# The gate and up product of a block by seven products of halves, with running sums in PSUM

## The chip, the cores and the metric

The kernel runs on one core of one Trainium2 chip. The metric is the device time of one launch in microseconds (us), as the median of several runs. The engines are TensorE (PE: matmuls; its weight loads are shown apart as PEld), VectorE (DVE), ScalarE (ACT), GpSimd (POOL) and SyncE (SP), which issues most of the DMA transfers. Everything is float32 except the grid of quantized values, which is bfloat16. A float32 matmul appears as two records on PE.

## The reference

The input is x of shape 4 x 2048 x 256. All of it is normalized, and two branches work on the normalized xn; their results are multiplied.

```python
xn = _layernorm(x)
# s: a linear attention layer
Q = elu(xn @ Wq + bq) + 1;  K = elu(xn @ Wk + bk) + 1;  V = xn @ Wv + bv     # 16 heads of 64
KV = einsum('bshd,bshm->bhdm', K, V)
Z = 1 / (einsum('bshd,bhd->bsh', Q, K.sum(axis=1)) + 1e-6)
o = einsum('bshd,bhdm,bsh->bshm', Q, KV, Z)
x1 = layer_norm(xn + o @ Wo + bo, g1, be1)
s = layer_norm(x1 + gelu(x1 @ W1 + b1) @ W2 + b2, g2, be2)
# g: a gated feed-forward layer whose operands are quantized to FP4 in blocks of 16
fp4_linear = lambda x, w: fp4_quant_dequant(x) @ fp4_quant_dequant(w).T
h = silu(fp4_linear(xn, w_gate)) * fp4_linear(xn, w_up)     # 704 wide
g = silu(fp4_linear(h, w_down))
out = x + s * g
```

A block of 16 values is quantized by its greatest magnitude: scale = max / 6, each value over the scale is rounded to the nearest of 0, 0.5, 1, 1.5, 2, 3, 4, 6, and multiplied by the scale again. The keys and values of a whole batch are needed before its first row of attention.

## The kernel before

**Blocks.** The 8192 rows are 32 blocks of 256 rows (`TB` = 2 halves of 128 rows, `j` = 0, 1), eight to a batch. The first part of the program reads the weights, quantizes those of the gated layer and works through the keys of batch 0. The main loop runs over the blocks n = 0 to 31. While the blocks of one batch are worked on, two sub-blocks of the keys of the next batch go along with each (`keys_k`, `keys_xk`): this holds for n = 0 to 23, the last batch (n = 24 to 31) has no such work. In the first half of a batch the keys' rows are normalized in the block before, in the second half they are loaded again from DRAM. Program step n multiplies the gate and up product of block n + 1 (`gate_up(n + 1)`, L753), because the quantization that must follow it takes most of a block.

**One block in order of TensorE.** Keys of the next batch (`pk`, `pxk`), then the gate and up product (`pg`), the down product of block n (`pd`), the first part of the second feed-forward product of block n - 1 (`py`) or more keys, the attention product (`pa`), the rest of the keys and of `py`; in between, the transposes of x1 (`pt_x`) and of the scales (`pscale`); then the queries of block n + 1 (`pq`), the first feed-forward product (`pf`) and the row sums of attention (`pz`). TensorE and all queues of DMA follow the program's order. ScalarE and VectorE instructions of the loop are placed by a scheduler that runs ahead of the launch; `tc.issue_after(x)` holds an instruction behind x. In the launch the order of each engine is fixed.

**The gate and up product** (`gate_up`, L753 to L776). The left side is the quantized xn of a block, transposed: `qT[:, NI + c, j*128 : (j+1)*128]` is the half c of the 256 contracted values, for the row half j. The right side `wgu` (L339) holds both weights side by side, 1408 columns for each c. For each j and each piece of 352 columns (`IH`), a gate tile and an up tile are accumulated over c = 0, 1: 16 matmuls of 128x352 in eight tiles of PSUM. ScalarE takes silu of the gate tile into h, VectorE multiplies h by the up tile. `mm_tile` (L89) gives out PSUM banks from a rotating pool of four (tag "mm"), `acc_tile` (L92) from a pool of two.

**After it.** `qz` (L865) multiplies the queries by the normalizing factor zb, in two halves of VectorE. zb comes through DRAM: `sums` (L838) writes the reciprocal z (`z_d`) and loads it four times, spread over partitions. The four loads are in SP's queue, behind what was issued before. `qz` is held behind `blk[n + 1]["late"]`, the third of the four multiplications that make h. Then `attention_sums` (the sums `zs`), the attention product `pa` and `add_seven` give x1, in `attention_norm` (L966) its statistics go to POOL for the power of -1/2 (L430) and x1 is normalized, and TensorE transposes it (`x1_T`, L971). In the last batch `pa` is a plain product, and x1 one add.

**The quantization of h** has a reduction of magnitudes (`scales_h`), its reciprocal and a multiplication (`fp4_scaled`), a magnitude by ScalarE (`m_h`), a rounding and a subtraction into `grid` (`fp4_rounded`), for each half j; `grid_T` transposes the grid by DMA, `spread_scales` sends the scales through DRAM to `qT`, and in the next step `quantized_h` and `quantized_x` multiply the two in `qT`.

**Seven products.** The attention and the second feed-forward product are already made by seven products of halves instead of eight (`seven_sums`, `seven_products`, `add_seven`, L889 to L922): sums of quarters of the left side, sums of quarters of the weights, each of the seven products in its own part of two banks, and the results added by VectorE.

**Values and keys of a half** (`m_of_half`, L608). Twice per batch, the sums of keys over 512 columns are multiplied by Wv (`wv`) and Wo. wv is loaded from DRAM or, for one half, kept from the first part in a tile of its own (`wv_sb`, L252).

Of the kernel before, what the change touches and what calls it, by code (L numbers as in the profile page):

```python
# [8 lines left out]
F32 = mybir.dt.float32  # L9
# [3 lines left out]
ALU = mybir.AluOpType  # L13
AX = mybir.AxisListType

P = 128
# [6 lines left out]
def linear_attention_gated_by_fp4_ffn(  # L23
# [230 lines left out]
    def load_wv(f, dep):  # L254
        wv_sb[f] = batch.tile([P, ND, HALF], F32, tag="wv", name=f"wv_{f}", bufs=1)
        load_when(dep, wv_sb[f], by_chunks(Wv)[:, :, f * HALF : (f + 1) * HALF])

    def wv_bias(f):
        bias_in_row0("v", wv_sb[f], f, nc.gpsimd)
        wv_d[f] = dram.tile([P, ND, HALF], F32, tag=f"wv_d{f}", name=f"wv_d{f}", bufs=1)  # L260
        nc.sync.dma_start(wv_d[f], wv_sb[f])
        if f > 0:
            del wv_sb[f]
# [75 lines left out]
    wgu = const.tile([P, ND, 2 * I], F32, name="wgu")  # L339
# [31 lines left out]
    def quantize_gu(ks):  # L371
# [14 lines left out]
        for i, k in enumerate(ks):  # L386
            pt = mm_tile(f"pwgu_{k}")
            for c in range(ND):
                lo = i * D + c * P
                tr(pt[:, c * P : (c + 1) * P], w[:, lo : lo + P], ident)  # L390
            scalar.copy(
                wgu[:, :, k * P : (k + 1) * P], pt[:, : ND * P].rearrange("p (c k) -> p c k", c=ND)
            )
# [214 lines left out]
    def m_of_half(b, f, dep=None, ahead=False):  # L608
# [3 lines left out]
        if wv_sb.get(f) is not None:  # L612
            wv = wv_sb.pop(f)
        else:
            wv = batch.tile([P, ND, HALF], F32, tag="wv", name=f"wv_{nm}", bufs=1)
            nc.sync.dma_start(wv, wv_d[f])
# [9 lines left out]
        xk = batch.tile([P, ND, HALF], F32, tag="xk", name=f"xk_{nm}", bufs=1)  # L626
# [115 lines left out]
    def quantized_x(n):  # L742

        qx = qT[:, NI:, :]
        t = gridT[n][:, NI * TB :, :].rearrange("p (c j) t -> p c (j t)", j=TB)
        return vector.tensor_tensor(qx, qx, t, ALU.mult)
# [6 lines left out]
    def gate_up(n):  # L753
        blk[n]["h"] = []
        for j in range(TB):
            h = work.tile([P, I], F32, tag="h", name=f"h_{n}_{j}")
            blk[n]["h"].append(h)
            for i in range(2):
                halves = []
                for part in range(2):  # L760
                    pg = mm_tile(f"pg_{n}_{j}_{i}_{part}")[:, :IH]
                    lo = part * I + i * IH
                    for c in range(ND):
                        mm(
                            pg, qT[:, NI + c, j * P : (j + 1) * P], wgu[:, c, lo : lo + IH],
                            start=c == 0, stop=c == ND - 1,
                        )
                    halves.append(pg)
                    if part == 0:
                        yield  # L770
                hh = h[:, i * IH : (i + 1) * IH]
                scalar.activation(hh, halves[0], AF.Silu)
                ins = vector.tensor_tensor(hh, hh, halves[1], ALU.mult)
                if (j, i) == (1, 0):
                    blk[n]["late"] = ins.ins
                yield  # L776
# [288 lines left out]
    for n in range(NB):  # L1065
# [52 lines left out]
        if n == 6:  # L1118
            load_xn(0)
# [10 lines left out]

    step(gate, 4)
    step(ready)
    step(m_0)
    scales_h(0, 0)
    scales_x(1)
    step(gate, 4)
# [33 lines left out]
    for n in range(NBLK):  # L1170
# [79 lines left out]
        if subs:  # L1250
            keys_xk(b + 1, subs[1])
            if subs[1] % NB == NB - 1:
                m_half = m_of_half(b + 1, subs[1] // NB)
                step(m_half)
# [29 lines left out]
        if n > 0:  # L1284
            ffn_2(n - 1, 28)
        if more[0]:
            q_of(n + 1)
# [74 lines left out]
```

## Time and profile before

| | before |
|---|---|
| median of 3 runs | 1878.16 us (1877.71 to 1878.72) |
| span of the profiled execution | 1880.7 us |
| granted clock of TensorE | 0.999 |
| PE busy | 1861.7 us, 99% |
| PEld (weight loads) busy | 1383.0 us, 74% |
| DVE busy | 1363.6 us, 73% |
| ACT busy | 706.7 us, 38% |
| POOL busy | 386.9 us, 21% |
| gate and up product, PE rows `pg` | 308.5 us in 1024 records |

The profile shows one execution, whose span of 1880.7 us stands 2.5 us above the median of the runs. A line of a group of instructions names the line of the kernel, the engine, the operation, the tile written and the tiles read, the number of instructions, then their busy time, the mean duration of one in ns, and the engine's idle time just before them with what ended it. L103 and L119 are the helpers through which all matmuls and all scheduled instructions of VectorE and ScalarE pass, so a group is known by its tiles. A line of the waits gives the waiting engine and tile, what it waited for, and then the total, the number of waits and the longest, in us. A line of the timeline gives start and duration in us, the engine, and how many instructions are merged into it; brackets give idle time before it and its releaser. Instructions on VectorE overlap slightly, so the pitch from one start to the next is a little shorter than a duration.

### The profile page before, as it was taken

Reading aid. Unit: us, or ns where it says so; the run is one execution under the profiler, and the core shown is the slowest. Engines: PE = TensorE matmul, PEld = TensorE weight load, DVE = VectorE, ACT = ScalarE, POOL = GpSimd, SP = SyncE. Lnnn points to the kernel's source line nnn. Section 1 sums busy time; section 2 is a strip of 40 time slices with the busy share of each in tenths; the row PEclk is TensorE's granted clock in tenths of the full one; section 3 lists DMA queues with packets and bytes.
Section 4 is the critical chain, followed back from the end, with each engine's and each line's share of the span. In section 5 each row is a group of like instructions: output and inputs, shape, how many; then the busy total and the mean of one; then the engine's idle time right before and its main releaser. Section 6 shows DMA issues by size and latency. Waiting matters only on the chain.

```text
span 1880.7 us, 25219 instructions
## 1 busy us (share of the span) xinstructions
PE 1861.7 (99%) x9324; PEld 1383.0 (74%) x9324; DVE 1363.6 (73%) x2526; ACT 706.7 (38%) x1191; POOL 386.9 (21%) x371
## 2 busy tenths in 40 slices
PE   9999999999999999999999999999999999999998
PEld 4456677777777777777677787777777788888887
DVE  5676777766677877777667787776676767777775
ACT  2333544333334335443233533353322333333332
POOL 1411322011122212220112221122101122222212
PEclk9999999999999999999999999999999999999999
DMA  5526564434535456635344544564543544444442
GB/s 184 193 73 130 117 124 103 96 101 94 96 64 94 115 98 122 143 66 111 80 89 79 117 100 103 96 139 87 95 86 72 104 75 87 82 90 83 88 84 54
DMA packets 229434, 188.78 MB, mean 100 GB/s; under 512 B 107687, under 2 KB 191155, under 8 KB 229310
## 3 DMA queue, kind: packets, MB, share of 16 engines
q1 hardware_dynamic: 228476, 185.58, 47.4%
q8 instruction: 74, 1.21, 0.3%
q10 hardware_dynamic: 834, 1.58, 0.3%
q14 instruction: 50, 0.41, 0.1%
HBM read 131.96 MB, written 32.59 MB: 87 GB/s over the span
## 4 chain that ended last, share of the span: by engine, by line
PE 78%; DVE 11%; DMA 7%; issue 1%; POOL 1%; SPq 1%; ACT 1%; POOLq 0%; ACTq 0%; DVEq 0%
PE pg L103 13%; PE pf L103 11%; PE pk L103 10%; PE pxk L103 10%; PE pq L103 9%; PE pa L103 8%; PE pd L103 7%; PE py L103 7%; DMA zb<-z_d 3%; PE pz L103 2%; DMA z_d<-z 1%; DVE y L119 1%; DMA xn<-xn_d 1%; DVE x L119 1%; DVE hs L119 1%
## 5 line engine op out<-in xcount | busy, mean ns | idle before, releaser
L430 POOL TENSOR_TENSOR rstd<-rstd,neg_half 128x2 f32<-128x2 f32 (+1 forms) x98 | 77.8, 795 | 1298.0 <-DVE rstd L119 984.9
L103 PE MATMUL pg<-wgu,qT 128*128 128x352 f32 x1024 | 308.5, 459 | 0.1
L103 PEld LDWEIGHTS pg<-wgu,qT 128*128 128x128 f32 x1024 | 194.3, 190 | 113.7 <-issue 11.5
L103 PE MATMUL pk<-wk_sb,xnT_k 128*128 128x512 f32 x512 | 230.4, 592 | 1.2 <-ACT xnT_k L119 1.2
L103 PE MATMUL pq<-xnT,wq_sb 128*128 128x256 f32 x1024 | 227.6, 380 | 1.5 <-DVE zq L119 1.4
L103 PE MATMUL pxk<-kk,xn_k 128*128 128x512 f32 x496 | 227.9, 598 | 1.0 <-DVE kk L119 1.0
L103 PE MATMUL pf<-x1T,w_sb 128*128 128x256 f32 x1024 | 227.2, 380 | 1.1 <-DVE zq L119 0.6
L103 PEld LDWEIGHTS pf<-x1T,w_sb 128*128 128x128 f32 x1024 | 193.8, 190 | 30.4 <-DVE zq L119 4.0
L103 PEld LDWEIGHTS pq<-xnT,wq_sb 128*128 128x128 f32 x1024 | 191.8, 190 | 27.7 <-DVE zq L119 3.1
L119 DVE SCALAR_TENSOR_TENSOR kk<-ek,pk 128x512 f32<-128x512 f32 x128 | 85.6, 685 | 173.2 <-ACT ek L119 173.2
L103 PE MATMUL pd<-wd,qT 128*128 128x256 f32 x768 | 172.9, 380 | 0.0
L103 PEld LDWEIGHTS pk<-wk_sb,xnT_k 128*128 128x128 f32 x512 | 97.0, 190 | 102.6 <-issue 89.0
L119 ACT ACT_TABLE_LOAD x121 | 155.2, 1283 | 40.9 <-PE pk L103 26.0
L119 ACT ACTIVATE x1T<-pt_x,bcol 128x256 f32<-128x256 f32 x64 | 32.7, 561 | 359.3 <-PE pt_x L106 359.3
L103 PEld LDWEIGHTS pd<-wd,qT 128*128 128x128 f32 x768 | 145.3, 190 | 26.4 <-issue 2.5
L103 PEld LDWEIGHTS pxk<-kk,xn_k 128*128 128x128 f32 x496 | 89.4, 190 | 99.1 <-issue 87.3
L119 DVE TENSOR_TENSOR h<-h,pg 128x352 f32<-128x352 f32 x128 | 66.1, 517 | 107.1 <-PE pg L103 104.0
L119 ACT ACTIVATE h<-pg 128x352 f32<-128x352 f32 x128 | 58.9, 460 | 209.8 <-PE pg L103 209.7
L119 ACT ACTIVATE hT<-pf,bcol 128x256 f32<-128x256 f32 x256 | 106.1, 472 | 66.7 <-PE pf L103 66.3
L119 DVE TENSOR_TENSOR zq<-zq,zb 128x1024 f32<-128x1024 f32 x64 | 78.9, 1232 | 68.9 <-DMA zb<-z_d 68.8
L103 PE MATMUL py<-w_sb,hs 128*128 128x128 f32 x992 | 122.0, 275 | 0.0
L119 ACT ACTIVATE e<-pq,neg_one 128x512 f32<-128x512 f32 x128 | 86.2, 685 | 83.7 <-PE pq L103 71.2
(161 smaller groups left out, 2777.8 us busy)
## 6 DMA issues: line engine op xcount, KB each, us to landing
zb<-z_d SPq DMA_DIRECT2D x128, 256.0 KB, 6.2
qT<-scale_d SPq DMA_DIRECT2D x248, 128.0 KB, 6.0
x_k<-in_L_attn_src_dram SPq DMA_DIRECT2D x32, 256.0 KB, 4.1
x<-in_L_attn_src_dram SPq DMA_DIRECT2D x32, 256.0 KB, 2.9
xn_d<-xn_k SPq DMA_DIRECT2D x32, 256.0 KB, 2.5
xn<-xn_d SPq DMA_DIRECT2D x32, 256.0 KB, 2.7
xnT_d<-xnT_k SPq DMA_DIRECT2D x32, 256.0 KB, 2.0
xnT<-xnT_d SPq DMA_DIRECT2D x32, 256.0 KB, 4.3
```

The source lines that it names most:

```text
L103: return tc.keep_in_program_order(nc.tensor.matmul(*args, **kw))
L119: ins = op(*args, **kw)
L430: pool["last"] = nc.gpsimd.tensor_tensor(rstd[:, j0:j1], rstd[:, j0:j1], neg_half[:, j0:j1], ALU.pow).ins
```

## The change

The product of a block is written as a product of 2 x 2 quarters: the left side has row halves and halves of the contracted values (`quarters_of`), the right side halves of the contracted values and gate or up, each 704 columns wide. Seven products of quarters replace eight, each for two pieces of 352 columns, 14 matmuls in place of 16. The left sides 3, 5, 6, 7 are sums `xs` that VectorE makes once a block, in a tile that shares its place with x1T. The sums of the weights (`gate_sums`) are made once by POOL; `wgu` keeps seven parts in place of four, and the copies into it are split at the border between gate and up.

The products are put together in PSUM where several outputs share a partial sum: two banks (`run`) hold product 1, ScalarE copies it out as the base of the gate's first half, product 6 is added onto it, ScalarE copies that out as the base of up, product 7 is added onto it, and at last product 4, which makes the gate's second half. A second pair of banks holds product 5, which ScalarE copies out, and then product 5 plus 3. A third allocation of two banks takes product 2. VectorE adds the pieces (`up`, in a tile that shares its place with `zs`). ScalarE takes silu of the first half of h from SBUF and of the second from PSUM. Both halves of h are complete only at the end of the product; `late` is now the last multiplication of the first half.

To make room, wv is no longer kept: each `m_of_half` loads it into a tile that it shares with xk and with zb, and the start's copy of Wv uses the tile of wo. `m_of_half` moves behind the last part of `ffn_2`, and in the first part the order of the last weight, the first gate product and the scales of x is changed.

```diff
@@ -252,15 +252,13 @@
     wv_sb, wv_d = {}, {}
 
     def load_wv(f, dep):
-        wv_sb[f] = batch.tile([P, ND, HALF], F32, tag="wv", name=f"wv_{f}", bufs=1)
+        wv_sb[f] = batch.tile([P, ND, HALF], F32, tag="wo", name=f"wv_{f}", bufs=1)
         load_when(dep, wv_sb[f], by_chunks(Wv)[:, :, f * HALF : (f + 1) * HALF])
 
     def wv_bias(f):
         bias_in_row0("v", wv_sb[f], f, nc.gpsimd)
         wv_d[f] = dram.tile([P, ND, HALF], F32, tag=f"wv_d{f}", name=f"wv_d{f}", bufs=1)
-        nc.sync.dma_start(wv_d[f], wv_sb[f])
-        if f > 0:
-            del wv_sb[f]
+        nc.sync.dma_start(wv_d[f], wv_sb.pop(f))
 
     cols = {}
 
@@ -336,7 +334,18 @@
         return x.rearrange("p (k e) -> p k e", e=BLK)
 
 
-    wgu = const.tile([P, ND, 2 * I], F32, name="wgu")
+    wgu = const.tile([P, 7, I], F32, name="wgu")
+    GU_OF = {"11": 0, "21": 1, "t1": 2, "22": 3, "t2": 4, "t3": 5, "t4": 6}
+
+    def wg(q):
+        return wgu[:, GU_OF[q], :]
+
+    def gate_sums():
+        nc.gpsimd.tensor_tensor(wg("t3"), wg("22"), wg("t1"), ALU.subtract)
+        nc.gpsimd.tensor_tensor(wg("t1"), wg("t1"), wg("11"), ALU.subtract)
+        nc.gpsimd.tensor_tensor(wg("t2"), wg("22"), wg("t1"), ALU.subtract)
+        nc.gpsimd.tensor_tensor(wg("t4"), wg("21"), wg("t2"), ALU.subtract)
+
     wd = const.tile([P, NI, D], F32, name="wd")
     nc.gpsimd.memset(wd[TAIL:, NI - 1, :], 0.0)
 
@@ -388,9 +397,15 @@
             for c in range(ND):
                 lo = i * D + c * P
                 tr(pt[:, c * P : (c + 1) * P], w[:, lo : lo + P], ident)
-            scalar.copy(
-                wgu[:, :, k * P : (k + 1) * P], pt[:, : ND * P].rearrange("p (c k) -> p c k", c=ND)
-            )
+            ptc = pt[:, : ND * P].rearrange("p (c k) -> p c k", c=ND)
+            lo, hi = k * P, (k + 1) * P
+            for part in range(2):
+                a, z = max(lo, part * I), min(hi, (part + 1) * I)
+                if a < z:
+                    scalar.copy(
+                        wgu[:, part * ND : (part + 1) * ND, a - part * I : z - part * I],
+                        ptc[:, :, a - lo : z - lo],
+                    )
         yield
 
     def load_down():
@@ -609,11 +624,9 @@
 
 
         nm = f"{b}_{f}"
-        if wv_sb.get(f) is not None:
-            wv = wv_sb.pop(f)
-        else:
-            wv = batch.tile([P, ND, HALF], F32, tag="wv", name=f"wv_{nm}", bufs=1)
-            nc.sync.dma_start(wv, wv_d[f])
+        t = work.tile([P, 2, ND, HALF], F32, tag="zb", name=f"wv_xk_{nm}", bufs=1)
+        wv, xk = t[:, 0], t[:, 1]
+        nc.sync.dma_start(wv, wv_d[f])
         wo = batch.tile([P, 4, D], F32, tag="wo", name=f"wo_{nm}", bufs=1)
         load_when(dep, wo, by_chunks(Wo)[:, 4 * f : 4 * f + 4, :])
         if ahead:
@@ -623,7 +636,6 @@
             nc.gpsimd.memset(kh[b], 0.0)
         m = m_sb[b, f] = batch.tile([P, 4, D], F32, tag=f"m{f}", name=f"m_{nm}", bufs=2 - f)
         pxk = keys.pop((b, "pxk", f))
-        xk = batch.tile([P, ND, HALF], F32, tag="xk", name=f"xk_{nm}", bufs=1)
         for d in range(ND):
             scalar.copy(xk[:, d, :], pxk[d])
 
@@ -743,7 +755,17 @@
 
         qx = qT[:, NI:, :]
         t = gridT[n][:, NI * TB :, :].rearrange("p (c j) t -> p c (j t)", j=TB)
-        return vector.tensor_tensor(qx, qx, t, ALU.mult)
+        vector.tensor_tensor(qx, qx, t, ALU.mult)
+        s = blk[n + 1]["xs"] = work.tile([P, 4, P], F32, tag="x1T", name=f"xs_{n + 1}", bufs=1)
+        h = quarters_of(qx)
+        vector.tensor_tensor(s[:, 0], h["21"], h["22"], ALU.add)
+        vector.tensor_tensor(s[:, 1], s[:, 0], h["11"], ALU.subtract)
+        ins = vector.tensor_tensor(s[:, 3], h["12"], s[:, 1], ALU.subtract)
+        vector.tensor_tensor(s[:, 2], h["11"], h["21"], ALU.subtract)
+        return ins
+
+    def quarters_of(t):
+        return {f"{j + 1}{c + 1}": t[:, c, j * P : (j + 1) * P] for j in range(TB) for c in range(ND)}
 
     def quantized_h(n, j):
 
@@ -751,29 +773,62 @@
         return vector.tensor_tensor(qh, qh, gridT[n][:, j * NI : (j + 1) * NI, :], ALU.mult)
 
     def gate_up(n):
-        blk[n]["h"] = []
-        for j in range(TB):
-            h = work.tile([P, I], F32, tag="h", name=f"h_{n}_{j}")
-            blk[n]["h"].append(h)
-            for i in range(2):
-                halves = []
-                for part in range(2):
-                    pg = mm_tile(f"pg_{n}_{j}_{i}_{part}")[:, :IH]
-                    lo = part * I + i * IH
-                    for c in range(ND):
-                        mm(
-                            pg, qT[:, NI + c, j * P : (j + 1) * P], wgu[:, c, lo : lo + IH],
-                            start=c == 0, stop=c == ND - 1,
-                        )
-                    halves.append(pg)
-                    if part == 0:
-                        yield
-                hh = h[:, i * IH : (i + 1) * IH]
-                scalar.activation(hh, halves[0], AF.Silu)
-                ins = vector.tensor_tensor(hh, hh, halves[1], ALU.mult)
-                if (j, i) == (1, 0):
-                    blk[n]["late"] = ins.ins
-                yield
+
+        h = blk[n]["h"] = [work.tile([P, I], F32, tag="h", name=f"h_{n}_{j}") for j in range(TB)]
+        t = work.tile([P, 4, IH], F32, tag="zs", name=f"up_{n}", bufs=1)
+        up = [[t[:, 2 * j + u] for u in range(2)] for j in range(TB)]
+        q, xs = quarters_of(qT[:, NI:, :]), blk[n]["xs"]
+        left = {
+            1: q["11"], 2: q["12"], 3: xs[:, 3], 4: q["22"], 5: xs[:, 0], 6: xs[:, 1], 7: xs[:, 2]
+        }
+        part = [slice(u * IH, (u + 1) * IH) for u in range(2)]
+
+        def product(i, bank, start):
+            for u in range(2):
+                mm(
+                    bank[u], left[i], wg(WEIGHT[i])[:, part[u]], start=start, stop=True,
+                    skip_group_check=True,
+                )
+
+        def banks(name):
+            return [mm_tile(f"{name}_{n}_{u}")[:, :IH] for u in range(2)]
+
+        run = banks("pg")
+        product(1, run, True)
+        for u in range(2):
+            scalar.copy(h[0][:, part[u]], run[u])
+        yield
+        other = banks("pg5")
+        product(5, other, True)
+        for u in range(2):
+            scalar.copy(up[1][u], other[u])
+        yield
+        product(6, run, False)
+        for u in range(2):
+            scalar.copy(up[0][u], run[u])
+        yield
+        product(3, other, False)
+        for u in range(2):
+            vector.tensor_tensor(up[0][u], up[0][u], other[u], ALU.add)
+        yield
+        product(7, run, False)
+        for u in range(2):
+            vector.tensor_tensor(up[1][u], up[1][u], run[u], ALU.add)
+        yield
+        last_ = banks("pg2")
+        product(2, last_, True)
+        for u in range(2):
+            hh = h[0][:, part[u]]
+            vector.tensor_tensor(hh, hh, last_[u], ALU.add)
+            scalar.activation(hh, hh, AF.Silu)
+            blk[n]["late"] = vector.tensor_tensor(hh, hh, up[0][u], ALU.mult).ins
+        yield
+        product(4, run, False)
+        for u in range(2):
+            hh = h[1][:, part[u]]
+            scalar.activation(hh, run[u], AF.Silu)
+            vector.tensor_tensor(hh, hh, up[1][u], ALU.mult)
+        yield
 
     def down(n, j):
         if j == 0:
@@ -1116,6 +1171,7 @@
         if n == 5:
             add_b2(dep)
         if n == 6:
+            gate_sums()
             load_xn(0)
             scales_x(0)
             spread_scales(-1, False, True)
@@ -1128,12 +1184,13 @@
     load_xn(1)
     load_xnT(0)
 
+    step(ready)
     step(gate, 4)
-    step(ready)
     step(m_0)
+    scales_x(1)
+    step(gate, 2)
     scales_h(0, 0)
-    scales_x(1)
-    step(gate, 4)
+    step(gate, 1)
     scales_h(0, 1)
     step(m_0, 2)
     m_half = m_of_half(0, 1)
@@ -1249,9 +1306,6 @@
             load_xn(n + 2)
         if subs:
             keys_xk(b + 1, subs[1])
-            if subs[1] % NB == NB - 1:
-                m_half = m_of_half(b + 1, subs[1] // NB)
-                step(m_half)
         bn, bin_ = divmod(n + 1, NB)
         next_subs = (2 * bin_, 2 * bin_ + 1) if bn + 1 < B else ()
         for sub in next_subs if n > 0 else ():
@@ -1283,6 +1337,9 @@
             spread_scales(n + 1, *more)
         if n > 0:
             ffn_2(n - 1, 28)
+        if subs and subs[1] % NB == NB - 1:
+            m_half = m_of_half(b + 1, subs[1] // NB)
+            step(m_half)
         if more[0]:
             q_of(n + 1)
         if n == 0:
```

## The prediction

> **What bounds the kernel now.** I read the page first (which engine is full, at which clock), then TensorE's and VectorE's waits, then the costs of the rows that the change touches, then two blocks in order of time. 0.2% of 1878 us, 3.8 us, is about what a measurement here can tell from no change.
>
> From the page: engines, and the granted clock.
>
> ```profile
> span 1880.7 us, 25219 instructions
> PE 1861.7 (99%) x9324; PEld 1383.0 (74%) x9324; DVE 1363.6 (73%) x2526; ACT 706.7 (38%) x1191; POOL 386.9 (21%) x371
> PEclk9999999999999999999999999999999999999999
> ...
> L103 PE MATMUL pg<-wgu,qT 128*128 128x352 f32 x1024 | 308.5, 459 | 0.1
> ...
> L119 DVE TENSOR_TENSOR h<-h,pg 128x352 f32<-128x352 f32 x128 | 66.1, 517 | 107.1 <-PE pg L103 104.0
> L119 ACT ACTIVATE h<-pg 128x352 f32<-128x352 f32 x128 | 58.9, 460 | 209.8 <-PE pg L103 209.7
> ```
>
> TensorE is full at full clock, so work taken from it is worth its time, if the work handed to the others is ready by then. VectorE has 27% free on average; the two lists of waits (PE's, then DVE's) say where.
>
> ```profile
> PE pa L103 <- DVE zs L119: 1.6, 4, 0.7
> ...
> PE pt_x L106 <- DVE x L119: 1.1, 3, 0.4
> ...
> DVE kk L119 <- ACT ek L119: 173.2, 81, 8.2
> DVE h L119 <- PE pg L103: 104.0, 60, 3.6
> DVE zq L119 <- DMA zb<-z_d: 68.8, 32, 6.6
> ```
>
> TensorE waits some 10 us in all. VectorE's free time lies early in a block: at the first keys (kk), inside the gate product (pg), and for zb. From zb until the block's end it hardly waits. Block 6, in order of time (DVE, then PE), shows that stretch; its gate product starts at 502.90:
>
> ```profile
> 508.46 0.89 DVE L119 TENSOR_REDUCE scale<-h 128x44 f32<-128x704 f32 x1
> ...
> 515.05 1.22 DVE L119 TENSOR_TENSOR zq<-zq,zb 128x1024 f32<-128x1024 f32 x1 [3.65 <-DMA zb<-z_d]
> ...
> 530.92 0.69 DVE L119 TENSOR_REDUCE scale<-xn 128x32 f32<-128x512 f32 x1 [1.08 <-DMA xn<-xn_d]
> ...
> 534.67 0.73 DVE L119 TENSOR_SCALAR x<-x,mv,rstd 128x256 f32<-128x256 f32 x2 [0.82 <-POOL rstd L430]
> ...
> 535.13 0.87 PE L106 MATMUL pt_x<-ident,x 128*128 128x128 f32 x4
> ```
>
> zb lands 12.15 us after the gate's start, x1 is normalized from 19.62 us after that, and TensorE transposes it (pt_x) 0.46 us later, at 32.23, the moment that it is free. There is no slack: in such a block VectorE's chain from zb and TensorE's work have the same length. A block of the last batch, 27 (gate from 1668.36):
>
> ```profile
> 1688.42 0.69 DVE L119 TENSOR_TENSOR x<-xn,pa 128x512 f32<-128x512 f32 x1 [0.67 <-PE pa L103]
> 1689.14 0.75 DVE L119 BATCH_NORM_STATS2 st<-x 128x6 f32<-128x256 f32 x2
> ...
> 1691.13 0.74 DVE L119 TENSOR_SCALAR x<-x,mv,rstd 128x256 f32<-128x256 f32 x2 [0.81 <-POOL rstd L430]
> ...
> 1691.79 0.68 PE L106 MATMUL pt_x<-ident,x 128*128 128x128 f32 x4
> ```
>
> Here x1 waits for TensorE, and statistics, power and normalization follow it without anything between: 3.37 us from x1 to pt_x.
>
> **The change, part by part.** Per block, 16 gate matmuls of 128x352 become 14. Each is two records; in block 6 the 32 records take 9.47 us, 0.592 a matmul. Two fewer: 1.184 us, in 32 gate products 37.9 us. This is the gain offered.
>
> *Copies.* ScalarE gets six copies of 128x352 a block; by the row of h<-pg 6 x 0.460 = 2.8 us, 88 us in all, in a gate stage where it was busy 1.84 of 9.47 us. *Sums.* VectorE gets six adds of 128x352 (h<-h,pg: 0.517 each, 3.1 us) and four of 128x128 for the left sides; the rows of 128x512 (0.682) and 128x256 (0.415) extended give an estimate of 0.28, 1.1 us together. 4.2 us a block, 135 in all: VectorE goes from 1364 to 1499, 80% of the span.
>
> *The waits inside the gate product.* With 0.592 a matmul, run (product 1) is done at 1.18 and copied by 1.7 and 2.2; the product that adds onto it begins at 2.37. The next pair gives the same: each copy or add has about 1.1 us to spare before the product that overwrites its bank. The sums fill VectorE's wait for pg and end, multiplications included, near 9.8 us. I take no stall. Bounds: the copies and the adds could each be late by one row's duration at the four turns where a bank is reused: 4 x 0.5 us x 32 = 64 us above; below, 0. I take 0, because the slack is two of these durations. Behind a waiting add stand only VectorE's next adds, the multiplications of h and qz; behind a waiting copy, ScalarE's next copy and silu. ScalarE's table load (1283 ns by its row) falls between the copies and silu, where it is hidden by products 3 and 7.
>
> [...] The trace here shows a granted clock of 0.999 over stages that already alternate banks by seven products (py, pa), so the sum goes by the row: nothing.
>
> *What leaves the gate stage.* Before, VectorE used its waits on pg for reducing and scaling the first half of h: 508.46 to 510.9, four instructions (0.89, 0.19, 0.43, 0.89). Running sums finish both halves of h only at the end, so these, 2.0 us at the pitch of their starts, move behind qz, onto the stretch without slack. This gives the gain back. By kind of block:
>
> - Keys reloaded (n = 3 to 6, 11 to 14, 19 to 22: 12 blocks). zb's landing is set by SP's queue, not by the gate, and stays. From zb to x1: +2.0 for the four, -0.43 for the multiplication of h that used to stand behind qz, -1.1 because they fill the wait for xn, about -0.2 at other small gaps: +0.3. TensorE arrives 1.18 earlier and waits 1.45, so the block gains nothing and loses 0.3. Where zb comes early (10.0 to 10.6 us: n = 3, 11, 19) the whole 1.15 is kept. Block by block: 3 x -1.15, and between -0.3 and +0.5 for nine others, together +1.75: -1.7.
> - Keys beside, first half of the next batch (10 blocks, n = 1, 2, 7 to 10, 15 to 18). zb comes at 9.65 and pt_x is in time, but of the moved work reciprocal, both scalings, rounding and grid (0.34 + 0.80 x 4 = 3.56) now stand around x1's sums and the statistics of the next keys, where waits of about 2.2 us take part of it. The first zq of q would finish at 39.98 after the gate's start, while TensorE wants that zq's bank at 38.56: a stall of 1.4 to 1.5 against 1.18 gained, +0.3 each: +2.9. (Gate tiles go from eight to six a block, so the rotation of four banks turns by two: this product then waits for zq where it waited for the last add of y.)
> - Last batch (7 blocks, n = 24 to 30). Between x1 and its normalization now stand rounding 0.80, grid 0.81 and one add of y 0.60, 2.2 us, of which the power's wait hides some 0.2: x1 to pt_x 5.3 instead of 3.37. x1 itself is early by 1.18, so pt_x is late by 0.72 against before in five blocks; in n = 27 and 26, where the second zb is late (11.75, 13.67), by 1.25 and 2.2: +7.1.
> - n = 23 -0.5, n = 0 nothing.
> - The start: gate 0 is 1.18 shorter, but xs and the last weight rounding (ended 126.97, product at 127.91) no longer lie under it, and the first grid of x ends about 2 us later: between -1.2 and +3; I take +1.3, the middle, as neither row decides.
>
> *The rest.* Four POOL sums of weight parts (128x704, once; by the 128x512 rows of 1.3 to 1.6 us some 8 us, before gate 0, while POOL is free): 0, up to +3 if they end late. Splitting the copies of the weight: one more copy: 0. Values' weights wv are loaded 512 KB per half batch instead of kept, behind PE's use of the shared tile on SP's queue, ahead of qT's scales; m_of_half moves behind ffn_2. It happens six times in the loop; DMA is about half loaded in the page's slices, at 100 GB/s. 0, up to +1 each, +6.
>
> Sum: -1.7 + 2.9 + 7.1 - 0.5 + 1.3 = +9.1 on the profiled 1880.7, which lies 2.5 us above the median of the runs (1878.16). 1889.8 - 2.5 = 1887; I say 1886, as the pitch of small instructions is rounded up in the sums.
>
> **Rivals.** *A, the gain is kept.* VectorE's waits (kk 173, zb 69 us) absorb the moved work, as the order is made new: 20 to 30 of the 37.9 us land. For it: the average of 20% free; zb waits 3.65 us in block 6. Against: that wait lies ahead of the stretch, not in it. If only the chains in the ten and seven blocks have slack, 17 x 1.18 + the kept 3.5 = 24 off: 1854; all of it gives 1840. It decides where the stalls of a block fall below 1.18 us: this rival ends faster.
> *B, ScalarE's copies or VectorE's adds stall the product inside the gate stage.* For it: four turns per gate with 1.1 us of slack, and a copy behind another ACT instruction (686 ns ek) has less. Against: ScalarE's queue is empty there in block 6. 0.3 us at each of four turns in 32 products: 38 on top, 1925; half of that 1906.
> *C, about equal.* Stalls equal the gain, 1.18 each, and the start costs nothing: 1878 to 1881.
>
> **How the numbers follow.** Forecast (chains give the gain back, +4 to +20): 0.50. A: 0.27, of which a third ends within 12 us of the time before. B or transfers late: 0.14. C: 0.09. Faster by over 0.2%: A, 0.27. Same: C and a small edge of the forecast, 0.10. Slower: 0.63. The range leaves out half of A below, at 1860, and the upper half of B, at 1908.
>
> **What would show it.** Right: PE busy falls by about 38 us, DVE rises to about 1490 to 1500, ACT to about 795; PE's waits grow from 10 to some 45 us, on pt_x <- x and pq <- zq, not on pg; in block 6 x1 is normalized 19.9 us after zb lands; in the last batch pt_x comes 5.3 us after x1. Wrong: waits at pg <- up or h (B), or TensorE's waits below 25 us with a span near 1855 (A), or a granted clock below 0.99.

## The result

The changed kernel takes 1929.31 us (median of four runs, 1925.96 to 1935.58), the kernel before 1878.26 beside it: the ratio is 1.0279, 95% interval 1.0258 to 1.0301. It is 51 us slower; 1886 had been forecast, with a range up to 1908. The profiled execution spans 1924.9 us, 44.2 more than that of before.

The page of the changed kernel, engines, clock and the new groups of the gate product:

```profile
span 1924.9 us, 25490 instructions
PE 1839.6 (96%) x9196; PEld 1363.7 (71%) x9196; DVE 1494.4 (78%) x2846; ACT 792.5 (41%) x1384; POOL 394.9 (21%) x375
PEclk9999999999999999999999999999999999999999
...
L103 PE MATMUL pg<-wgu,xs 128*128 128x352 f32 x512 | 157.4, 460 | 2.3 <-DVE z L119 2.3
L103 PE MATMUL pg<-wgu,qT 128*128 128x352 f32 x384 | 124.6, 460 | 1.4 <-DVE up L119 1.4
```

The added work has the size that was worked out: VectorE 1494 us, ScalarE 793. The gate product is as quick as forecast: block 6 has it from 515.45 to 523.73, 8.28 us against 9.47, and its groups wait 3.7 us in the whole run. But TensorE is 22 us less busy, not 38, and it is idle for 85 us (19 before); its waits add up to 78 us, where some 45 had been forecast. The head of its list of waits says behind what:

```profile
PE pt_x L106 <- DVE x L119: 28.7, 16, 2.5
PE pq L103 <- DVE zq L119: 19.6, 10, 3.0
PE pa L103 <- DVE zq L119: 7.2, 9, 1.5
PE pscale_-1_833 L106 <- DVE scale L119: 3.6, 1, 3.6
PE pa L103 <- DVE zs L119: 3.5, 5, 1.2
PE pz L103 <- DMA kh<-k_d: 3.4, 3, 1.7
```

All of these but the last are waits for VectorE. The starts of the gate products cut the profiled execution into stages (us; the sums of the differences are the 44.2):

| stage | before | after | forecast | measured |
|---|---|---|---|---|
| up to the first gate product, and it and its stage | 161.06 | 167.76 | +1.3 | +6.7 |
| block 0 | 54.58 | 53.44 | 0 | -1.1 |
| keys beside, 10 blocks | 572.57 | 589.31 | +2.9 | +16.7 |
| keys reloaded, 12 blocks | 691.35 | 693.46 | -1.7 | +2.1 |
| block 23 | 53.34 | 53.06 | -0.5 | -0.3 |
| last batch, to the end | 347.80 | 367.87 | +7.1 | +20.1 |

Block 6, in order of time on VectorE and then TensorE, answers the stretch shown of before:

```profile
527.09 1.23 DVE L119 TENSOR_TENSOR zq<-zq,zb 128x1024 f32<-128x1024 f32 x1 [1.85 <-DMA zb<-z_d]
529.96 1.23 DVE L119 TENSOR_TENSOR zq<-zq,zb 128x1024 f32<-128x1024 f32 x1 [1.65 <-DMA zb<-z_d]
...
540.03 0.89 DVE L119 SCALAR_TENSOR_TENSOR h<-h,rs_h 128x704 f32<-128x704 f32 x1
541.29 0.89 DVE L119 SCALAR_TENSOR_TENSOR h<-h,rs_h 128x704 f32<-128x704 f32 x1
...
548.40 0.74 DVE L119 TENSOR_SCALAR x<-x,mv,rstd 128x256 f32<-128x256 f32 x2 [0.81 <-POOL rstd L445]
...
548.87 0.87 PE L106 MATMUL pt_x<-ident,x 128*128 128x128 f32 x4 [1.53 <-DVE x L119]
```

zb lands 11.64 us after the gate's start, a little earlier than before, x1 is normalized 21.31 us after it (19.62 before), and TensorE, early by the two matmuls, stands 1.53 us for it. VectorE stands 1.85 us for the first part of zb and 1.65 us for the second, with the reduction and scaling of h still to do behind them. The 21.31 us are 1.4 more than the 19.9 forecast, and the second of these waits is in no term of the sum. That the wait of pt_x comes out near the 1.45 us forecast is in part luck: zb landed 0.5 us earlier, and TensorE arrived some 0.8 us later than forecast.

Block 27, where the difference is the greatest of the last batch (+5.7), on VectorE, POOL and TensorE:

```profile
1695.28 1.51 DVE L119 TENSOR_TENSOR xs<-qT 128x128 f32<-128x128 f32 x2
1696.72 1.35 DVE L119 TENSOR_TENSOR xs<-xs,qT 128x128 f32<-128x128 f32 x1
1698.11 1.25 DVE L119 TENSOR_TENSOR xs<-qT,xs 128x128 f32<-128x128 f32 x1
...
1695.18 1.26 POOL L863 TENSOR_TENSOR o<-g,be_r 128x512 f32<-128x512 f32 x1
1696.52 1.41 POOL L864 TENSOR_TENSOR o<-o,x 128x512 f32<-128x512 f32 x1
1697.88 1.32 POOL L865 TENSOR_TENSOR g<-g,g_r 128x512 f32<-128x512 f32 x1
...
1725.22 0.87 PE L106 MATMUL pt_x<-ident,x 128*128 128x128 f32 x4 [2.48 <-DVE x L119]
...
1728.79 7.76 PE L103 MATMUL pq<-xnT,wq_sb 128*128 128x256 f32 x32
```

Before, the same product of queries took:

```profile
1694.53 7.07 PE L103 MATMUL pq<-xnT,wq_sb 128*128 128x256 f32 x32
```

Two things stand here that the forecast did not have. Three of the four xs take 1.25 to 1.35 us each beside POOL's additions, so that the four last 4.1 us from start to end; in the first three batches, block 1 apart, the four took 1.0 us. And the 32 records of pq after the wait take 7.76 us instead of 7.07: the granted clock was 0.50 from 1726.77 to 1730.18 us.

### The profile page after: what moved, and what is told of

The parts are those of the page before. It is cut to its first block, busy times and chain, and to the rows that moved or that the text cites. A ratio compares the mean times of both kernels' runs of the same rounds, so it can differ in the third digit from the quotient of the medians.

```text
span 1924.9 us, 25490 instructions
## 1 busy us (share of the span) xinstructions
PE 1839.6 (96%) x9196; PEld 1363.7 (71%) x9196; DVE 1494.4 (78%) x2846; ACT 792.5 (41%) x1384; POOL 394.9 (21%) x375
## 4 chain that ended last, share of the span: by engine, by line
PE 42%; DVE 28%; DMA 21%; SPq 3%; POOL 2%; ACT 2%; issue 2%; DVEq 0%; POOLq 0%; ACTq 0%
DMA zb<-z_d 8%; PE pf L103 8%; PE pk L103 7%; PE pq L103 6%; PE pxk L103 6%; PE pg L103 5%; DVE hs L119 3%; DVE scale L119 3%; DMA xn<-xn_d 3%; DMA z_d<-z 3%; PE py L103 3%; PE pd L103 3%; DVE h L119 3%; DVE zq L119 2%; DVE x L119 2%; DMA gridT<-grid 2%
## 5 line engine op out<-in xcount | busy, mean ns | idle before, releaser
L103 PE MATMUL pq<-xnT,wq_sb 128*128 128x256 f32 x1024 | 231.5, 383 | 19.7 <-DVE zq L119 19.6
L119 ACT ACT_TABLE_LOAD x121 | 155.2, 1283 | 36.7 <-PE pk L103 21.5
L103 PE MATMUL pg<-wgu,xs 128*128 128x352 f32 x512 | 157.4, 460 | 2.3 <-DVE z L119 2.3
L103 PEld LDWEIGHTS pg<-wgu,xs 128*128 128x128 f32 x512 | 97.2, 190 | 57.2 <-DVE z L119 3.9
L103 PE MATMUL pg<-wgu,qT 128*128 128x352 f32 x384 | 124.6, 460 | 1.4 <-DVE up L119 1.4
L119 ACT ACTIVATE m_h<-h 128x704 bf16<-128x704 f32 x64 | 50.9, 795 | 174.0 <-DVE h L119 174.0
```

The lines of the kernel that those rows point to most:

```text
L103: return tc.keep_in_program_order(nc.tensor.matmul(*args, **kw))
L119: ins = op(*args, **kw)
```

## The experiments

Theory V: VectorE's static order sets the blocks, above all what stands behind zb; TensorE's 1.18 us a block are worth their time only where that chain has slack. Against it: P, TensorE still sets the time and the loss comes from the start, from VectorE slowed beside POOL and from the clock; and N, VectorE is simply full.

**TensorE's saving alone.** In the kernel before, one contraction half of the last gate piece is left out, which makes 14 matmuls and adds nothing (`...` stands for lines left out, here and below):

```diff
-                    for c in range(ND):
+                    nd = 1 if (j, i) == (1, 1) else ND
+                    for c in range(nd):
...
```

> The kernel before with two matmuls fewer per gate product: the last piece takes only one half of the contracted values (so the output is another one); nothing else is changed. It asks what TensorE's 1.18 us a block is worth by itself. Theory V (VectorE's chain from zb is as long as TensorE's work in the blocks with reloaded keys): 12 blocks gain nothing, the others 1.18 us each, 20 x 1.18 = 24 us, near 1855 us. Rival P (TensorE alone sets the time): all 37.9 us, 1840 us. Rival N (VectorE sets it everywhere): within 8 us of 1878.

Measured: 1857.66 us, ratio 0.9881 (0.9866 to 0.9896), 21.5 us off. By stages: keys beside -9.6, last batch -7.7, the twelve reloaded blocks -2.5 of the 14.2 offered. So even without any added work the two matmuls were worth 21.5 us of 37.9, and in the reloaded blocks hardly anything. That is near the 1855 that V gave, and far from P and N.

**The saving undone in the changed kernel.** Product 4 is added twice:

```diff
         product(4, run, False)
+        product(4, run, False)
```

> The changed kernel with product 4 added onto its banks twice (the output is another one): TensorE has its 1.18 us a block again, everything on VectorE and ScalarE stays. Theory V (the chains of VectorE set the blocks of the changed kernel): 0 to 12 us more than 1929. Rival P (TensorE's time is on the path): 38 us more, 1967 us.

Measured: 1938.00 us, ratio 1.0317 (1.0296 to 1.0337), 8.7 us above the changed kernel for 37.9 us of matmuls (7 by the two ratios, whose intervals overlap). TensorE's waits shrank in their place:

```profile
PE pt_x L106 <- DVE x L119: 20.4, 16, 2.1
PE pz L103 <- DMA kh<-k_d: 5.2, 3, 2.5
PE pq L103 <- DVE zq L119: 4.3, 5, 2.0
```

The wait of pq went from 19.6 to 4.3, that of pt_x from 28.7 to 20.4. P is out: most of TensorE's added time disappears in waits that it had anyway.

**The move of the scaling alone.** In the kernel before, the reduction of the first half of h is held behind qz, and with it its scaling:

```diff
-            scales_h(n + 1, 0)
+            with tc.issue_after(qz_ins):
+                scales_h(n + 1, 0)
```

> The kernel before, with 16 matmuls and no sums, copies or xs; only the reduction of the first half of h is held behind qz, so that its scaling leaves the gate stage as in the changed kernel. It asks what this move alone costs. Theory V (the moved 2.0 to 3.6 us stand on VectorE's chains): 12 to 30 us more than 1878, with waits of pt_x for x in the last batch. Rival (the added sums and xs make the chains late, the moved work finds free time): 0 to 4 us.

Measured: 1908.44 us, ratio 1.0150 (1.0129 to 1.0170): 29 us, with no product changed. By stages: reloaded blocks +15.8, last batch +9.4, keys beside +1.5. The head of its list of waits has pt_x, as in the changed kernel, but no pq:

```profile
PE pt_x L106 <- DVE x L119: 19.2, 15, 2.8
PE pscale L106 <- DVE scale L119: 4.2, 6, 1.4
```

This is the greatest cost that one part of the change has by itself, and it adds no work at all. It does not account for every stage: in the blocks with keys beside, where the change loses 16.7 us, the move alone costs 1.5, and in the reloaded blocks it costs 15.8, where the whole change loses 2.1. So its 29 us are not simply a part of the 51.

**The weights of the values, alone.** The kernel before with wv loaded for each half into the tile of zb, and `m_of_half` behind the last part of `ffn_2`:

```diff
...
-        if wv_sb.get(f) is not None:
...
+        t = work.tile([P, 2, ND, HALF], F32, tag="zb", name=f"wv_xk_{nm}", bufs=1)
+        wv, xk = t[:, 0], t[:, 1]
+        nc.sync.dma_start(wv, wv_d[f])
...
```

> The kernel before with one part of the change alone: the weights of the values loaded for each half batch into the tile shared with zb, and the half's product moved behind the last part of the feed-forward product; same output. Theory: this has a price of its own, the wait of pz for kh (0.7 to 2.4 us in blocks 7, 15 and 23), 2 to 7 us in all: 1880 to 1885. Rival: the loads delay qT's scales on SP's queue too, 10 us or more. Or nothing: 1878.

Measured: 1884.10 us, ratio 1.0032 (1.0019 to 1.0045), 5.8 us. The wait of pz for kh is there, 3.7 us in three blocks.

**The sums of weights at the start.** The four sums on POOL are left out, and the three weight parts that only they fill are set to zero early:

```diff
...
         if n == 6:
-            gate_sums()
```

> The changed kernel without the four sums of weights on POOL; the three tiles that only they fill are set to zero early (the output is another one). In the trace these sums ran from 109.6 to 118.0 us, VectorE's instructions beside them took up to 1.1 us longer each, TensorE stood 3.58 us for the scale and its clock fell. Theory S (POOL's sums hold VectorE): first gate product 6 to 7 us earlier, 1922 us. Rival (the new order of the start does it): 0 to 1 us.

Measured: the first gate product starts at 127.81 us instead of 135.04. In four other runs that have the sums at the same place (e2, e4, e6, e7) it starts at 133.4 to 134.0, so the sums cost 5.6 to 7.2 us there. This is how they did it in the changed kernel, on POOL, VectorE and TensorE, and then the two rows of before:

```profile
111.85 2.20 POOL L345 TENSOR_TENSOR wgu<-wgu 128x704 f32<-128x704 f32 x1
...
112.55 2.24 DVE L119 TENSOR_TENSOR w_down<-w_down,am_wd 128x704 f32<-128x704 f32 x1
115.31 1.03 DVE L119 TENSOR_SCALAR rstd<-mv 128x2 f32<-128x2 f32 x1
...
116.57 0.45 PE L106 MATMUL pscale_-1_833<-ident,scale 128*128 128x128 f32 x1 [3.58 <-DVE scale L119]
116.81 8.15 PE L103 MATMUL pk<-wk_sb,xnT_k 128*128 128x512 f32 x12
```

```profile
111.53 0.89 DVE L119 TENSOR_TENSOR w_down<-w_down,am_wd 128x704 f32<-128x704 f32 x1
...
113.52 5.32 PE L103 MATMUL pk<-wk_sb,xnT_k 128*128 128x512 f32 x12
```

The VectorE instruction of 128x704 took 0.89 us before, and one of 128x2 0.16; TensorE stood 3.58 us, and then 12 records of pk took 8.15 us, the granted clock being 0.50 from 115.68 to 122.50 us, before 5.32 at 1.00. But the whole took 1931.77 us, ratio 1.0283 (1.0266 to 1.0301): none of the 7.2 us reached the end. In the profile the stage of the first gate product and block 0 gave back 3.5, the blocks with keys 4.1; why is not settled.

**POOL's addends behind the xs**, in the last batch:

```diff
             ins = quantized_h(n, 0)
-            gpsimd_behind(qT[:, 0, :])
+            with tc.issue_after(ins.ins):
+                ins = quantized_x(n)
+            gpsimd_behind(blk[n + 1]["xs"][:, 2])
             gate_addend(n - 1)
             block_addends(n)
-            with tc.issue_after(ins.ins):
-                ins = quantized_x(n)
```

> The changed kernel with POOL's three addend instructions of the last batch held behind the four xs instead of behind the first product of h, same output. In the trace the xs took 2.9 us there against 1.1 elsewhere. Theory S (POOL beside VectorE stretches both engines' pairs): xs back at 1.1 us, z and zb 1.8 us earlier in seven blocks, 8 to 13 us off, 1918 us. Rival (zb's time is not what makes x1 late, only the moved work of h does): 0 to 3 us off.

Measured: 1924.93 us, ratio 1.0244 (1.0228 to 1.0259), 4.4 us off, less than forecast. The tile that POOL waits for is not the last that VectorE writes: the first three xs are back at 0.28 us, the last still takes 1.38. The last batch is 5.4 us shorter; in four runs that leave it as it is (e2, e3, e6 and the changed kernel) it differs by 1.9 us at most, so the direction is shown. The size is about half of what Theory S gave.

**The adds of y ahead of the rounding of h** in the blocks with keys beside:

```diff
...
+            first = output_sums(n - 1) if n > 0 and next_subs and bin_ in (2, 3, 0, 1) else None
-            grid_of_h(n + 1, 1, blk[n]["act"])
+            grid_of_h(n + 1, 1, blk[n]["act"], first)
```

Here `output_sums` is the call of `add_seven` out of `output`, and `first` holds the rounding behind its last add.

> The changed kernel, same output, with the five adds of the second feed-forward result (s, from the banks py) put ahead of the rounding of the second half of h on VectorE, in the blocks with keys beside. The fourth product of q then takes the bank of py instead of waiting for the first zq. Theory V: the waits of pq for zq (19.6 us in ten blocks) go or shrink below 5, 8 to 17 us off, 1912 to 1921 us. Rival (VectorE is simply full there and the wait moves to the next product): 0 to 4 us off.

Measured: 1917.61 us, ratio 1.0195 (1.0161 to 1.0228), 11.7 us off, with runs from 1908 to 1923. The wait of pq for zq is gone from the list:

```profile
PE pt_x L106 <- DVE x L119: 29.2, 17, 2.5
PE pa L103 <- DVE zq L119: 7.0, 10, 1.3
PE pf L103 <- DVE zq L119: 6.0, 9, 1.2
```

The ten blocks went from 589.3 to 575.3 us, and the wait of pf that is next in line is 6 us. In block 8 the fourth product of q starts 40.46 us after the gate's start, before the first zq ends (43.25); in the changed kernel it started at 43.81, just behind the first zq, and the last add of y came after that. So it was the order of five adds and one rounding, not a full engine.

**x1 first in the last batch**: the scaling and rounding of h are held behind the normalization of x1.

```diff
-            grid_of_h(n + 1, 0)
+            with tc.issue_after(blk[n]["normal"]) if not subs else nullcontext():
+                grid_of_h(n + 1, 0)
...
```

The same holds the second half.

> The changed kernel, same output, with the scaling and rounding of h in the last batch held behind the normalization of x1. Theory V (what stands between x1 and its normalization makes pt_x late): x1 to pt_x 3.4 us instead of 5, the wait of 2.48 us of pt_x in six blocks goes; but 3.3 to 4 us of h's work move towards the quantization that the next gate product waits for: between 14 us off and 5 more, 1915 to 1934. Rival (zb alone is late): no change.

Measured: 1935.25 us, ratio 1.0287 (1.0263 to 1.0311), nothing gained. The wait of pt_x is gone in the last batch, and another has its place:

```profile
PE pq L103 <- DVE zq L119: 19.9, 10, 3.0
PE pt_x L106 <- DVE x L119: 15.1, 13, 1.8
PE pscale L106 <- DVE scale L119: 13.4, 7, 2.0
```

pscale transposes the scales of x, whose reduction now stood behind the scaling of h. Work that is held back must be held behind everything that TensorE asks for in that stretch, not behind one tile of it.

**Four together**: e6 and e7, POOL's addends behind the last of the xs (also in block 1), and the sums of weights behind the first grid of x, by one element that POOL reads from it.

> The changed kernel, same output, with e6 and e7, POOL's addends behind the last xs (also in block 1), and the sums of weights on POOL behind the grid of x at the start. If the parts add: start -6, block 1 and last batch -12, keys beside -8 to -17, x1 first -14 to +5: 1880 to 1905 us. If VectorE is full and the waits only move: 1915 us or more.

Measured: 1907.86 us, ratio 1.0146 (1.0130 to 1.0162), just above the forecast of parts that add. pscale still waits 13.6 us, nearly all in the last batch.

**The scaling ahead of qz where zb is late.** e8, with the first half of h reduced and scaled before qz in the blocks of the second half of a batch and the last batch, and in the last batch the scale of x ahead of the rounding of h and the second half of h no longer held:

```diff
+        early = n < last and (not subs or (n > 0 and subs[1] >= NB))
+        if early:
+            scales_h(n + 1, 0)
+            blk[n + 1]["m_h", 0] = fp4_scaled(h3, blk[n + 1].pop(("rs_h", 0)), h3, f"h_{n + 1}_0")
+            hold = scaled[f"h_{n + 1}_0"]
-        with tc.issue_after(blk[n + 1]["late"]) if n < last else nullcontext():
+        with tc.issue_after(hold) if n < last else nullcontext():
             qz_ins = qz(n)
...
```

> e8 with the first half of h reduced and scaled ahead of qz instead of behind it, in the blocks with reloaded keys and in the last batch (where VectorE stands 1.4 to 2.3 us for zb after the gate product), and in the last batch with the scale of x ahead of the rounding of h; same output. Theory V (what counts is which work stands behind zb, not how much there is): the waits of pt_x and pscale in these blocks shrink from 28 to below 10 us, 15 to 25 us off e8's 1908: 1883 to 1893 us. Rival (VectorE is simply full): less than 6 us off e8.

Measured: 1896.55 us, ratio 1.0102 (1.0083 to 1.0121), 11.3 off e8: the direction of V, but below the 15 to 25 that it gave. The reloaded blocks, where only the scaling moved, are 8.3 us shorter than in e8 and 5 under the kernel before; the last batch, which has all three edits, stands at +6.0 instead of +16.2.

**Its two corrections**: of the blocks with keys only those whose zb is late (3 to 6 of each batch), and in the last batch only the reduction and the reciprocal ahead.

```diff
-        early = n < last and (not subs or (n > 0 and subs[1] >= NB))
+        early = n < last and (not subs or bi in (3, 4, 5, 6))
...
```

> e9 with two corrections: among the blocks with keys beside only those whose zb is late (n = 3 to 6 of each batch) scale the first half of h ahead of qz, and in the last batch only its reduction and reciprocal stand ahead (0.89 + 0.19 + 0.43 us), as zb lands there before 12.1 us and e9's attention product waited 1.45 us for it; same output. Theory V: blocks 3, 11, 19 lose their wait at pt_x (3 x 1.4), blocks 7, 15, 23 get their 12.88 us of qz back, the last batch up to 1.45 us in six blocks: 6 to 16 us off e9's 1897, 1881 to 1891 us, still not below the kernel before at 1878. Rival (these waits only move): 1895 to 1898.

Measured: 1888.97 us, ratio 1.0067 (1.0047 to 1.0087). TensorE's list of waits has no pt_x at its top any more:

```profile
PE pa L103 <- DVE zs L119: 11.0, 11, 1.8
PE pa L103 <- DVE zq L119: 9.1, 12, 1.5
PE pz L103 <- DMA kh<-k_d: 6.4, 3, 2.7
```

The reloaded blocks are 9.8 us shorter than before the change, of 14.2 offered; the last batch is still 8.3 longer, the blocks with keys beside 5.9. With the same seven products and the same sums, 40 us of the 51 came back by the order of VectorE's and POOL's instructions alone, and the kernel before is still 0.7% faster.

## Why the prediction was wrong

- In the profiled execution the forecast missed by 35 us: 13.8 in the blocks with keys beside, 13.0 in the last batch, 5.4 at the start, 3.8 in the reloaded blocks. The steps that failed are below: an x1 that was to come early, xs and weight sums priced by rows taken without POOL beside them, an order of the adds of y on VectorE that was not foreseen, and no term for the clock.
- *Direction and mechanism* were right: VectorE's chain behind zb and its order give the saving back, and inside the gate product hardly anything waits (3.7 us, in steps 0, 1 and 27). Rival B named 1925 us, but its mechanism did not occur: pg waited 1.4 us for up in the whole run, and for no copy of ScalarE.
- *"I take no stall" in the gate product*: right. ScalarE's six copies end before the table load (at 519.67 in block 6), as forecast.
- *Keys reloaded*, -1.7: +2.1. The wait of pt_x was forecast as 1.45 and is 1.3 to 1.6 in nine blocks. The three blocks whose zb was to come early (3, 11, 19) kept nothing; there zb landed at 11.9 to 12.1 us instead of 10.0 to 10.6. That zb's landing "stays" was wrong there. The "+0.3" from zb to x1 was wrong too: in block 6 it was +1.7 (21.31 against 19.62).
- *Last batch*, +7.1: +20.1. x1 to pt_x was forecast as 5.3 us and is 5.02. The step that failed is "x1 itself is early by 1.18": it is 0.5 to 2.9 us late, since qz can start on zb only 10.5 to 12.5 us after the gate's start in blocks 25 to 30, before 8.4 to 10.5. With the two matmuls fewer and nothing added (e1) x1 is indeed 1.19 us early in blocks 25 and 28 to 30, so what the change adds and moves makes it late. The term that was mis-sized is the four xs, 1.1 us by an estimate from rows without POOL beside them; beside POOL's addends they took 3.0 to 4.1 us. e4 and e8 show a part of this; e5 has 9.4 us in this batch from the moved scaling alone, in the kernel before.
- *Keys beside*, +2.9: +16.7. The stall of pq was there, 1.15 to 3.0 us in ten blocks against 1.4 to 1.5. Block 1 alone lost 6.1: its xs took 3.9 us beside POOL. Blocks 7 and 15 have the wait for kh, where the forecast had put "up to +1". And the reason given for pq's bank, a rotation that turns by two tiles, was wrong: e6 has the same number of tiles and only the order of the adds of y changed, and there the product no longer waits for zq. The bank that a product takes is not in the trace; that it goes by the order in which VectorE frees the banks is inferred from e6 alone.
- *The start*, +1.3: +6.7. "While POOL is free" was the failed step: POOL was free, but VectorE beside it was slowed (its 128x704 instruction took 2.24 us instead of 0.89), and without the sums the gate product came 7.2 us earlier (e3).
- *The clock*: the sum took nothing, because the trace of before had full clock (1.00 from 60 to 1868 us) through stages that alternate banks. It still has it there after the change: none of the 32 gate products fell below full clock, so nothing was right for them. But half clock came with three of the waits that the change makes (3.58, 2.04 and 2.48 us), and the prediction had no term for that: before the program's end 13.7 us at half clock in the profiled execution, which is 6.8 us lost by the granted clock.
- The single parts, each on the kernel before (or by the first gate product): -21.5 (e1), +29.3 (e5), +5.8 (e10), +7.2 (e3), together +21, or +14 without the start's 7.2, which did not reach the end. The remaining 30 to 37 of 51 us are left to the sums, the xs, the order of the adds of y (11.7 by e6) and the clock; they were not all measured one by one, and the parts need not add.

## What to carry to other kernels

Before work is taken from a full engine, ask stage by stage whether a chain of another engine has the same length; where it has, the saving is worth nothing, and leaving the work out is the cheap way to see that (21.5 of 37.9 us here). When a change finishes a tile later, follow every instruction that used to run in that stage's idle time: its new place cost 29 us by itself although nothing was added. An idle engine (POOL) is no free place for work if a busy one (VectorE) slows down beside it, as here, where xs took 0.9 to 1.4 us instead of 0.28.

## What was not expected of the hardware

**VectorE beside POOL.** In the changed kernel 22 of the 28 xs that ran beside an addition of POOL took 0.9 to 1.4 us instead of 0.28. The 44 `o<-s,rstd,o` of 128x256 that did took 1.47 to 1.49 us, the other 18 0.48; the six `y<-xn,rs_x` of 128x512 took 1.66 to 1.77 us, the other 26 0.66 to 0.69. POOL's additions of 128x512 in block 27 took 1.26 to 1.41 us. Not every instruction was hit: the seven adds `up<-up,pg` beside POOL, with one operand in PSUM, kept their 0.51, and two `zq<-zq,zb` their 1.22. Block 1 of e9, VectorE and POOL:

```profile
224.72 5.90 DVE L119 TENSOR_TENSOR h<-h,up 128x352 f32<-128x352 f32 x4
230.55 3.42 DVE L119 TENSOR_TENSOR zq<-zq,zb 128x1024 f32<-128x1024 f32 x2
...
225.67 1.56 POOL L219 TENSOR_TENSOR w_sb<-w_sb 128x512 f32<-128x512 f32 x1
227.31 1.43 POOL L220 TENSOR_TENSOR w_sb<-w_sb 128x512 f32<-128x512 f32 x1
228.82 1.43 POOL L221 TENSOR_TENSOR w_sb<-w_sb 128x512 f32<-128x512 f32 x1
```

The four multiplications of h take 1.99 us without POOL (block 6 of the changed kernel), 5.90 here. The price in these rows was some 1 us for each of these multiplications, two thirds of the 1.43 to 1.56 us of the POOL instruction beside it. An instruction with one operand was hit too: the 128x2 one at the start of the changed kernel took 1.03 us instead of 0.16.

**The clock after short waits.** The granted clock of the changed kernel in windows of 4 us (the columns behind the busy times are the granted clock, the DMA share and GB/s):

```profile
112.00:116.00 4.00, 0.99 (x3) 0.16 (x1) 4.00 (x5) 0.00 (x0) 3.92 (x2) 0.96 0.17 66
116.00:120.00 4.00, 3.43 (x5) 1.62 (x6) 3.35 (x5) 0.89 (x2) 3.92 (x4) 0.50 0.07 18
120.00:124.00 4.00, 4.00 (x8) 1.65 (x7) 2.82 (x6) 1.35 (x3) 0.38 (x1) 0.69 0.45 149
...
1724.00:1728.00 4.00, 2.78 (x18) 2.59 (x19) 3.74 (x8) 1.70 (x3) 2.44 (x3) 0.85 0.26 49
1728.00:1732.00 4.00, 4.00 (x17) 3.53 (x17) 4.00 (x3) 2.67 (x4) 3.00 (x2) 0.73 0.18 45
```

The granted clock is 0.50 from 115.68 to 122.50 us, which begins inside the wait of 3.58 us, and from 1726.77 to 1730.18, which begins 1.5 us after the end of the wait of 2.48; a third stretch, from 265.86 to 269.28, begins 0.6 us after the end of a wait of pq of 2.04. From 60 us on and without the last 12 us, TensorE has 12 waits of 2 us or more in this trace. Three of them came with half clock, and nine did not, among them one of 3.00, one of 2.63 and five of 2.48 to 2.49; none of the nine between 1.5 and 2 us did. In the kernel before the longest wait between 60 and 1868 us is 1.23 us, and the clock is 1.00. In windows of 2 us all thirteen profiles have 48 such stretches in that range, none in the kernel before and in e10, 11 in e7. By the granted clock 45 of them cost 1.7 us of full speed each and three 3.4.

What differs between two waits of the same length can be read from the trace of the changed kernel. Its three stretches start 44 and 428 steps of 3.413 us apart; in the eight other profiles with more than one, the starts lie on such steps too, to within 0.04 us. Divided into steps from 115.68 us, this trace has 538 of them at full clock from 60 us on and without the last 12 us. TensorE was busy for 21, 40 and 45% of the three ahead of the stretches, and for 47% or more of the other 535, which half clock did not follow. The wait of 2.04 us lay within one step, the one with 40%. The wait of 3.00 us was shared by two, with 49 and 63%, and half clock did not follow. This is one trace; where the border lies in others it does not show.

The runs of the changed kernel spread from 1926 to 1936 us with mean clocks of 0.990 to 0.996, those of the kernel before beside it over 1 us (0.999 in its profile); in the later sets the kernel before spread from 1877 to 1882 us at 0.998 to 1.000.
